# A graph-network kernel on one Trainium2 core: the first mixer's key sums taken apart from its queries

## The chip, the cores and the metric

The kernel runs on one core of one Trainium2 chip. The metric is device microseconds from launch to the end, lower is better. The program is one launch: five engines (TensorE, VectorE, ScalarE, GpSimd, SyncE; in the profile PE, DVE, ACT, POOL, SP) each work through their own instruction list in order and wait for each other by semaphores.

## The reference, cut to what matters

The network has two layers over 3125 nodes of 256 features (25 tiles of 128 nodes, the last one partly filled) and 53125 edges. Only the first layer's first step is touched by the change:

```python
xn = layernorm(x)
x = x + gnn(xn, src, dst, edge_weight) + mixer(xn)       # first layer, first step
x = x + experts(layernorm(x))                            # first layer, 32 experts, one chosen per node
# second layer: relational attention over the edges, a second mixer, a routed network
```

The graph part sums, for each node, `xn[src] * edge_weight` over its edges and multiplies by a weight. The mixer makes `q, k, v` from `xn`, norms q and k over the features and squares them, norms again (the keys' second norm is over the nodes, so it is known only when all nodes are summed), and needs `k.T @ v` over all nodes before any node's result is known:

```python
q2, k2 = square(norm(q)), square(norm(k))     # norm over a node's features
out = (q2 / |q2| per node) @ (k2.T @ v / |k2| per feature) @ W_out
```

The sum over nodes does not depend on the order of the nodes.

## The kernel before

**The head (`prepare`).** The nodes are read in node order (`xs`, 25 tiles). The head finds each node's first edge and its number of edges and sorts the nodes by it: the rank is called the node's *place*. The search runs in five rounds: VectorE makes row numbers (L969 to L973), GpSimd issues five indirect DMAs for them (L976), VectorE counts in what they brought (L980). Then comes one chain of VectorE and TensorE steps (L991 to L1039). Beside all this, the layernorm of each tile `xn` is made (L115 to L119) and written to a table `xtab` in HBM (L1045). The head ends with a flag that all engines load, and a branch: an engine enters the next stage only when its part of the head is done.

**The front (`front`).** After the branch, tile t holds the nodes of places 128t to 128t+127. GpSimd first gathers two edge windows (L1273) and the node rows by place (`xs`, L1570). Weights are loaded through ScalarE's DMA queue: 4 MB for the experts, then those of the mixer, its biases `b_qkv` last. Three streams are then woven together in the order of the program; ScalarE, VectorE and TensorE keep exactly this order (`manual_schedule`), while GpSimd's is set by the scheduler:

- `first_mixer`, a pipeline over 25 tiles. Per tile: layernorm (`norm1`, `norm2`), the transpose of `xn` (`turn`), three products (`products`: queries 256 wide, keys and values 512 wide, a direct part 256 wide), the norms and squares (`squares1`, `squares2`), and `sums`: the transpose of `q2` into `q2T`, `kvT += v.T @ k2` and `sqs += k2*k2`. It yields twice per tile. After the last tile come the scale `cn` and the matrix `kvo` (L1531 to L1547).
- `summing` (called `slots`): the graph part. A tile has as many *slots* as its node with the most edges, `SLOTS = [38, 25, 23, 22, 21, 20, 20, 19, 19, 18, 18, 17, ...]`, 444 in all. One step takes four slots: four indirect DMAs on GpSimd (L1384, tile `g`, four buffers of four slots) and four multiply-adds on VectorE (L1389, L1391). Two more steps per tile transpose the sum and multiply it by the weight (L1399 to L1403).
- `sources` (called `counts`): lists for the last network of the second layer, 32 blocks of 6 steps, mainly VectorE (L1151 to L1194).

The weaving in the mixer is this:

```python
while step is not None:
    at += 1
    if at > 6:
        slots()
        counts(step)      # the mixer yields 0, 1, 0, 1, ...: every second time
    step = next(mixer, None)
```

Then the experts run over 7 groups of four tiles (`chosen`, `experts`, `projections`). A group has 32 half steps. Each calls `more`, which makes one step of `slots` (at most up to the end of the group after next), issues one indirect scatter of the finished lists on GpSimd (L1240, two once all slots are done) and makes one step of `counts`. Before a group's experts start, `slots(NT * 99, ...)` finishes all slots of that group and of the next: the first group needs tiles 0 to 7. Lists can be scattered only when 8 blocks of `counts` are complete.

**The second layer** follows the front: gathers of `kvtab` (L1929), attention, and the routed network.

Of the kernel before, what the change touches and what calls it, by code (L numbers as in the profile page):

```python
# [12 lines left out]
F32 = mybir.dt.float32  # L13
BF16 = mybir.dt.bfloat16
I32 = mybir.dt.int32
AF = mybir.ActivationFunctionType
OP = mybir.AluOpType
# [4 lines left out]
P = 128  # L22
N = 3125
D = 256
KB = D // P
NT = 25
NP = NT * P
# [4 lines left out]
E2 = 32768  # L32
C2 = E2 // P
NTAB = 2
TR = NP + P
# [12 lines left out]
GS = 40  # L48
# [3 lines left out]
def rows(t):  # L52
    return P if t < NT - 1 else LAST
# [843 lines left out]
class Fast(Net):  # L897
# [32 lines left out]
    def prepare(self, ctx):  # L930
        tc, nc, a = self.tc, self.nc, self.a
        keep = ctx.enter_context(tc.tile_pool(name="pr_keep", bufs=1, reuse_waits="tile"))
# [8 lines left out]
        self.place = keep.tile([P, 2, NT], F32, name="place_of")  # L941
        flag = keep.tile([1, 1], I32, name="flag")
        self.ones3 = keep.tile([3, P], BF16, name="ones3")
        nc.vector.memset(self.ones3, 1.0)
        self.later = keep.tile([3, 2], F32, name="later")
        for k in range(2):
            nc.vector.tensor_scalar(self.later[:, k:k + 1], self.iotap[:3], float(k), -1.0, op0=OP.is_gt,
                                    op1=OP.mult)
        with ExitStack() as ctx:
# [7 lines left out]
                           allow_small_or_imprecise_dtypes=True)  # L957
# [82 lines left out]


            for t in range(NT):
                xn = work.tile([P, D], F32, name="xn")
                self.layernorm(work, self.xs[:, t, :], xn)
                nc.sync.dma_start(self.xtab[t * P:(t + 1) * P, :], xn)  # L1045
        return nc.values_load(flag, min_val=0, max_val=2 * P)

# [62 lines left out]
    def sources(self, ctx):  # L1110

        tc, nc, a = self.tc, self.nc, self.a
        B = 8
# [11 lines left out]
        slot = one.tile([P, C2], F32, name="slot2")  # L1125
        over = one.tile([P, C2], F32, name="over2")
        other = one.tile([P, C2], F32, name="other2")
        nc.gpsimd.iota(other, pattern=[[P, C2]], base=NP * GS, channel_multiplier=1,
                       allow_small_or_imprecise_dtypes=True)
        self.placed_chunks = 0  # L1130
# [15 lines left out]
        for b in range(C2 // B):  # L1146
# [48 lines left out]
            if b % 8 == 7:  # L1195

                cs = slice((b - 7) * B, (b + 1) * B)
                nc.vector.tensor_scalar(over[:, cs], slot[:, cs], float(GS), None, op0=OP.is_ge)
                nc.vector.scalar_tensor_tensor(slot[:, cs], dst[:, cs], float(GS), slot[:, cs],
                                               op0=OP.mult, op1=OP.add)  # L1200
                nc.vector.tensor_sub(other[:, cs], other[:, cs], slot[:, cs])
                nc.vector.tensor_mul(other[:, cs], other[:, cs], over[:, cs])
                nc.vector.tensor_add(self.sidx2[:, cs], slot[:, cs], other[:, cs])
                self.placed_chunks = (b + 1) * B
# [26 lines left out]
    def source_lists(self, n, to=None):  # L1231
# [7 lines left out]
        for c in range(len(done), min(len(done) + n, self.placed_chunks)):  # L1239
# [11 lines left out]
            done.append(ins)  # L1251
        self.last_scatters = done[-NCH:]

    def neighbours(self):
# [150 lines left out]

    def first_mixer(self, ctx, q2T, nq, kvo):

# [29 lines left out]
        kvT = ps.tile([P, KB, D], F32, name="kvT")  # L1437
        sqs = big.tile([P, D], F32, name="sqs")
        nc.vector.memset(sqs, 0.0)
        sd = {}  # L1440
        made = {}
        squared = {}
        xns = {}
        xTs = {}

        def norm1(t):
# [17 lines left out]
        def products(t):  # L1464
            xT = xTs.pop(t)
            pqv = ps.tile([P, 2, D], F32, name="pqv", bufs=2)
            pkv = ps.tile([P, 2 * D], F32, name="pkv", bufs=2)
            self.mm_rows(pqv[:, 0], xT, w_q, b_qkv[:, 0:D])
            self.mm_rows(pkv, xT, w_kv, b_qkv[:, D:])
            self.mm_rows(pqv[:, 1], xT, w_vo, b_vo)  # L1470
            made[t] = pqv, pkv

        def squares1(t):

            pqv, pkv = made[t]
            st = work.tile([P, 2, 6], F32, name="mx_st")
            mv = work.tile([P, 2, 2], F32, name="mx_mv")
            r = work.tile([P, 3, 2], F32, name="mx_sd")
            nc.vector.bn_stats(st[:, 0, :], pqv[:, 0])
            nc.vector.bn_stats(st[:, 1, :], pkv[:, 0:D])  # L1480
            for k in range(2):
                nc.vector.bn_aggr(mv[:, k, :], st[:, k, :])
            nc.scalar.activation(r[:, 0, :], mv[:, :, 1], AF.Sqrt, bias=self.eps[:, 1:2],
                                 scale=float(D))
            made[t] = pqv, pkv, mv, r

        def squares2(t):
            pqv, pkv, mv, r = made.pop(t)
            nc.vector.reciprocal(r[:, 1, :], r[:, 0, :])
            nc.vector.scalar_tensor_tensor(r[:, 2, :], mv[:, :, 0], -1.0, r[:, 1, :],  # L1490
                                           op0=OP.mult, op1=OP.mult)
            q2 = work.tile([P, D], F32, name="q2")
            k2 = work.tile([P, D], F32, name="k2")
            v = work.tile([P, D], F32, name="v")
            sq = work.tile([P, 2, D], F32, name="sq", bufs=2)
            nc.scalar.activation(q2, pqv[:, 0], AF.Square, bias=r[:, 2, 0:1], scale=r[:, 1, 0:1])
            nc.scalar.activation(k2, pkv[:, 0:D], AF.Square, bias=r[:, 2, 1:2],
                                 scale=r[:, 1, 1:2])
            nc.scalar.copy(v, pkv[:, D:])
            nc.vector.tensor_add(self.xs[:, t, :], self.xs[:, t, :], pqv[:, 1])  # L1500
            nc.scalar.activation(sq[:, 0, :], q2, AF.Square, accum_out=nq[:, t:t + 1])
            nc.scalar.activation(sq[:, 1, :], k2, AF.Square)
            squared[t] = q2, k2, v, sq

        def sums(t):
            q2, k2, v, sq = squared.pop(t)
            r = rows(t)
            self.transpose_to(ps, q2, q2T[:, :, t * P:(t + 1) * P])
            for k in range(KB):
                nc.tensor.matmul(kvT[:, k, :], v[:r, k * P:(k + 1) * P], k2[:r, :],  # L1510
                                 start=(t == 0 and k == 0), stop=(t == NT - 1 and k == KB - 1))
            nc.vector.tensor_add(sqs[:r], sqs[:r], sq[:r, 1, :])

        def there(f, t):
            if 0 <= t < NT:
                f(t)

        for t in range(-2, NT + 2):
            there(turn, t + 1)
            there(sums, t - 2)  # L1520
            there(products, t)
            there(norm1, t + 2)
            there(squares1, t - 1)
            yield 0
            there(norm2, t + 2)
            there(squares2, t - 1)
            yield 1

        kv = big.tile([P, KB, D], F32, name="kv")
        for k in range(KB):  # L1530
            nc.vector.tensor_copy(kv[:, k, :], kvT[:, k, :])  # L1531
        cn = work.tile([1, D], F32, name="cn")
        csum = ps.tile([1, D], F32, name="pqv", bufs=2)
        nc.tensor.matmul(csum, self.ones[:, 0:1], sqs, start=True, stop=True)
        nc.scalar.activation(cn, csum, AF.Sqrt)
        nc.vector.tensor_scalar_max(cn, cn, 1e-12)
        nc.vector.reciprocal(cn, cn)
        pc = ps.tile([P, KB], F32, name="pqv", bufs=2)
        for k in range(KB):
            nc.tensor.matmul(pc[:, k:k + 1], cn[:, k * P:(k + 1) * P], self.ones[0:1, 0:1],  # L1540
                             start=True, stop=True)
        rc = work.tile([P, KB], F32, name="rc")
        nc.vector.tensor_copy(rc, pc)
        for c in range(KB):
            pw = ps.tile([P, D], F32, name="pqv", bufs=2)
            self.mm_rows(pw, kv[:, :, c * P:(c + 1) * P], w_o)
            nc.vector.tensor_scalar(kvo[:, c, :], pw, rc[:, c:c + 1], None, op0=OP.mult)  # L1547
        nc.scalar.activation(nq, nq, AF.Sqrt)
# [4 lines left out]
    def front(self, q2T, qT, kvtab, own):  # L1553
# [5 lines left out]
        with ExitStack() as ctx:  # L1559
# [3 lines left out]
            nq = big.tile([P, NT], F32, name="nq")  # L1563
            kvo = big.tile([P, KB, D], F32, name="kvo")
            w_y = self.load_kb(big, "w_y", a["gcn_wT"])
# [29 lines left out]
            def counts(n=1):  # L1595
                for _ in range(n):
                    next(counted, None)

            self.edges_of(0)
            with ExitStack() as mctx:  # L1600
                mixer = self.first_mixer(mctx, q2T, nq, kvo)
                step = next(mixer)
                mctx.enter_context(tc.manual_schedule(
                    engines={mybir.EngineType.Activation, mybir.EngineType.DVE, mybir.EngineType.PE}))
                at = 0
                while step is not None:
                    at += 1
                    if at > 6:
                        slots()
                        counts(step)  # L1610
                    step = next(mixer, None)
# [821 lines left out]
```

## Time and profile before

| what | value |
|---|---|
| median of 17 runs | 2488.05 us (2483.55 to 2495.62) |
| the profiled execution | 2488.35 us, its span 2486.6 us |
| head, up to the flag (L1039) | 0 to 98.8 us |
| first norm of a query tile (L1479) | 149.55 us |
| last slots step before the experts (L1403, tile 7) | 453.46 us |
| first activation of the experts (L1709) | 456.14 us |
| first gather of the second layer (L1929) | 1258 us |

A line of the profile names the source line, the engine, what is written from what, and the shapes; `x444` is a count. "Busy" is the time that an engine executes; the idle time before an instruction is put down to what released it. PEclk is the granted clock of TensorE. In the timetables of stretches, the columns are the length and then, for each engine, busy time and number of instructions.

### The profile page before, as it was taken

How to read it: one execution, taken by the hardware profiler on the slowest of the kernel's cores; microseconds unless marked ns; L12 is line 12 of the kernel's file. 1: busy time of each engine (PE TensorE's matmuls, PEld its weight loads, DVE VectorE, ACT ScalarE, POOL GpSimd, SP SyncE). 2: the span in 40 equal slices, each digit the busy share in tenths (PEclk: the TensorE clock that was granted, in tenths of full speed). 3: DMA queues.
4: the chain of work that ended last, by engine and by line, in shares of the span. 5: the costliest groups of instructions: out<-in, count | busy, mean ns of one | idle time of the engine just before them, and what ended most of it. 6: DMA issues, size and time to landing. Idle time of an engine off the chain costs nothing.

```text
span 2486.6 us, 25047 instructions
## 1 busy us (share of the span) xinstructions
PE 1786.7 (72%) x7318; PEld 1113.9 (45%) x7318; DVE 1480.9 (60%) x4053; ACT 783.2 (31%) x2273; POOL 1588.5 (64%) x1675
## 2 busy tenths in 40 slices
PE   0177785677887889999837565756575658888898
PEld 0034443444444545555525343534354425555556
DVE  6566768866666565531468687978677823122227
ACT  1023331111121212222306443535454423332342
POOL 3376556777777776467357777767654037777764
PEclk9998886888899899999968776778767669999999
DMA  4443223432333332101167576756655031111101
GB/s 148 130 136 113 83 80 113 120 88 86 104 97 100 94 98 78 43 18 35 38 176 208 152 215 201 215 175 202 191 143 164 12 98 17 17 17 9 17 10 53
DMA packets 121375, 254.50 MB, mean 102 GB/s; under 512 B 36594, under 2 KB 61926, under 8 KB 120972
## 3 DMA queue, kind: packets, MB, share of 16 engines
q0 software_dynamic: 82656, 196.67, 28.5%
q1 hardware_dynamic: 31688, 49.09, 5.9%
q10 hardware_dynamic: 6884, 7.04, 1.0%
q8 instruction: 60, 0.98, 0.2%
q14 instruction: 87, 0.71, 0.1%
HBM read 228.93 MB, written 23.76 MB: 102 GB/s over the span
## 4 chain that ended last, share of the span: by engine, by line
POOL 13%; DVE 10%; PE 10%; issue 8%; DMA 5%; ACT 4%; DVEq 0%; POOLq 0%; ACTq 0%
POOL ed L2140 7%; DMA kv<-kvtab,src 4%; POOL kv L1929 3%; ACT kv L1966 3%; DVE kv L1937 2%; DVE kv L1935 2%; PE po L2279 2%; PE pu L1968 2%; PE ph L2267 2%; DVE sc L1938 2%; PE pz L926 1%; DMA ed<-htab,nb 1%; POOL hx L2107 1%; PE pr L1368 1%; PE pT L126 1%
## 5 line engine op out<-in xcount | busy, mean ns | idle before, releaser
L1384 POOL DMA_INDIRECT g<-xtab,src x444 | 445.1, 1002 | 188.0 <-issue 108.8
L1929 POOL DMA_INDIRECT kv<-kvtab,src x444 | 431.0, 971 | 183.0 <-issue 99.9
L2140 POOL DMA_INDIRECT ed<-htab,nb x279 | 265.0, 950 | 85.0 <-issue 81.0
L1240 POOL DMA_INDIRECT gl<-gsrc,sidx x256 | 255.8, 999 | 79.1 <-issue 76.8
L1966 ACT ACTIVATE kv<-kv,sc 128x64 f32<-128x64 f32 x1196 | 288.2, 334 | 21.5 <-DVE sc L1950 21.4
L1968 PE MATMUL pu<-kv,ident 128*128 128x256 f32 x888 | 259.1, 434 | 11.8 <-ACT kv L1966 9.9
L1391 DVE SCALAR_TENSOR_TENSOR acc<-g,wt,acc 128x256 f32<-128x256 f32 x419 | 202.8, 484 | 61.6 <-DMA g<-xtab,src 51.0
L2267 PE MATMUL ph<-xT,w 128*128 128x512 f32 (+1 forms) x448 | 191.1, 581 | 35.9 <-ACT h L2269 26.5
L1706 PE MATMUL ph<-xT,w 128*128 128x512 f32 (+1 forms) x448 | 214.8, 605 | 0.0
L1723 PE MATMUL po<-w,h 128*128 128x256 f32 x800 | 204.6, 397 | 0.0
L1968 PEld LDWEIGHTS pu<-kv,ident 128*128 128x128 f32 x888 | 175.6, 214 | 59.6 <-ACT kv L1966 37.2
L2279 PE MATMUL po<-w,h 128*128 128x256 f32 x800 | 187.0, 386 | 0.0
L2279 PEld LDWEIGHTS po<-w,h 128*128 128x128 f32 x800 | 148.9, 191 | 33.4 <-issue 15.4
L1723 PEld LDWEIGHTS po<-w,h 128*128 128x128 f32 x800 | 148.4, 196 | 34.2 <-issue 17.6
L1935 DVE TENSOR_TENSOR kv<-kv,pr 128x1024 f32<-128x1024 f32 (+3 forms) x121 | 133.2, 1123 | 46.6 <-DMA kv<-kvtab,src 32.0
L1709 ACT ACTIVATE h<-ph,b 128x512 f32<-128x512 f32 (+1 forms) x112 | 71.7, 640 | 265.0 <-PE ph L1707 265.0
L2267 PEld LDWEIGHTS ph<-xT,w 128*128 128x128 f32 x448 | 84.1, 201 | 124.6 <-issue 94.6
L1354 PE MATMUL pT<-typT,sel 18*128 18x128 bf16 (+9 forms) x229 | 32.1, 270 | 149.0 <-DVE typT L1345 146.9
L1937 DVE TENSOR_TENSOR kv<-kv,q 128x1024 f32<-128x1024 f32 (+3 forms) x121 | 132.3, 1122 | 0.0
L1938 DVE TENSOR_REDUCE sc<-kv 128x16 f32<-128x1024 f32 (+3 forms) x121 | 132.1, 1119 | 0.0
L1368 PE MATMUL pr<-self.relb,ohT 128*128 128x128 bf16 x687 | 79.2, 268 | 46.2 <-DVE ohT L1357 37.6
L1706 PEld LDWEIGHTS ph<-xT,w 128*128 128x128 f32 x448 | 82.2, 206 | 55.4 <-issue 53.9
(443 smaller groups left out, 2947.7 us busy)
## 6 DMA issues: line engine op xcount, KB each, us to landing
dr<-in_gat_dst_row SPq DMA_DIRECT2D x32, 512.0 KB, 3.9
g<-xtab,src POOLq DMA_INDIRECT x444, 2.8
kv<-kvtab,src POOLq DMA_INDIRECT x444, 3.7
own<-xq SPq DMA_DIRECT2D x25, 256.0 KB, 2.0
xq<-own SPq DMA_DIRECT2D x25, 256.0 KB, 3.2
ed<-htab,nb POOLq DMA_INDIRECT x279, 2.4
w<-in_ex_w ACTq DMA_DIRECT2D x2, 2048.0 KB
gl<-gsrc,sidx POOLq DMA_INDIRECT x256, 2.1
```

The lines of the kernel that those rows point to most:

```text
L1240: ins = nc.gpsimd.indirect_dma_start(out=self.gl[:, :], out_offset=bass.IndirectOffsetOnAxis(ap=self.sidx2[:, c:c + 1], axis=0), in_=self. ...
L1384: self.moved = nc.gpsimd.indirect_dma_start(out=g[:, s % 4, :], out_offset=None, in_=self.xtab[:, :], in_offset=bass.IndirectOffsetOnAxis( ...
L1391: nc.vector.scalar_tensor_tensor(acc, g[:, s % 4, :], self.wts[t][:, s:s + 1], acc, op0=OP.mult, op1=OP.add)
L1706: nc.tensor.matmul(ph[:, :n], w1[:, k, mc], xT[:, k, :n], start=(k == 0), stop=False)
L1723: nc.tensor.matmul(pos[j // 2][:, j % 2], this[:, j * P:(j + 1) * P], w2[:, m, :], start=False, stop=(m == M - 1 and (j % 2 == 1 or j == w ...
L1929: nc.gpsimd.indirect_dma_start(out=kv[:, j, :], out_offset=None, in_=kvtab[:, :], in_offset=bass.IndirectOffsetOnAxis(ap=self.srcs[t][:, g ...
L1935: nc.vector.tensor_tensor(k4, k4, rr[:, r0:r0 + n].unsqueeze(2).to_broadcast([P, n, 4, HD]), op=OP.add)
L1966: nc.scalar.activation(v[:, h * HD:(h + 1) * HD], v[:, h * HD:(h + 1) * HD], AF.Copy, scale=sc[:, s, h:h + 1])
L1968: nc.tensor.matmul(pu, self.ident, v, start=(s == 0), stop=(s == SLOTS[t] - 1))
L2140: nc.gpsimd.indirect_dma_start(out=ed[:, s, :], out_offset=None, in_=self.htab[:, :], in_offset=bass.IndirectOffsetOnAxis(ap=self.nbrs[t][ ...
L2267: nc.tensor.matmul(ph[:, :w], w1[:, e, k, m * P:(m + 1) * P], xT[:, :len(ts), k, :], start=(k == 0), stop=(k == KB - 1))
L2279: nc.tensor.matmul(po[:, i], hs[i][:, m, j * P:(j + 1) * P], w2[:, e0 + i, m, :], start=False, stop=(i == 1 and m == M - 1))
```

## The change

The mixer's keys no longer go with its queries. Since the sum over the nodes takes them in any order, the keys and values of the first 12 tiles in node order are made and summed in the head, next to the layernorm that makes `xn` there; the sums are kept in `kvs` and `cs`. After the branch the mixer first reads back `xtab` for node tiles 12 to 24, makes their keys and adds their sums. Only then do the queries run, by places, over all 25 tiles. The columns' squares are now summed by a matmul (`csum`) and no longer by VectorE (`sqs`). The scale and `kvo` (now in `kvs`) are made in four steps during the queries. The weaving changes: the mixer yields 0 twice per key tile, then 1 and 2 per query tile; every yield makes a step of `counts`, and only a 2 makes a step of `slots`.

The weights `w_kv` and the key biases are loaded once more for the head. Of the buffers of `sources`, two small ones are made anew every 8 blocks.

```diff
+NHEAD = 12
 # prepare
+            w_kv = self.load_kb(one, "w_kv", a["mix0_wkv"])
+            b_kv = self.load_terms(one, one, "b_kv", a["mix0_b"][D:])
+            def keys(t, xn):
+                xT = work.tile([P, KB, P], F32, name="xT", bufs=2)
+                self.transpose_to(ps, xn, xT)
+                pkv = ps.tile([P, 2 * D], F32, name="pkv", bufs=2)
+                self.mm_rows(pkv, xT, w_kv, b_kv)
...
+                r = self.key_norm(work, pkv)
+                self.key_squares(pkv, r, k2, v, sq)
+                return k2, v, sq
             for t in range(NT):
-                xn = work.tile([P, D], F32, name="xn")
+                xn = work.tile([P, D], F32, name="xn", bufs=8)
                 self.layernorm(work, self.xs[:, t, :], xn)
                 nc.sync.dma_start(self.xtab[t * P:(t + 1) * P, :], xn)
+                if t < NHEAD:
+                    now = t, *keys(t, xn)
+                if last:
+                    self.key_sums(kvT, csum, *last, 0, NHEAD - 1)
+            nc.scalar.copy(self.kvs, kvT)
+            nc.scalar.copy(self.cs, csum)
 # new helpers
+    def key_norm(self, work, pkv):
+        nc.vector.bn_stats(st, pkv[:, 0:D])
+        nc.vector.bn_aggr(mv, st)
+        nc.scalar.activation(r[:, 0:1], mv[:, 1:2], AF.Sqrt, bias=self.eps[:, 1:2], scale=float(D))
+        nc.vector.tensor_copy(r[:, 3:4], mv[:, 0:1])
+    def key_squares(self, pkv, r, k2, v, sq):
+        nc.vector.reciprocal(r[:, 1:2], r[:, 0:1])
+        nc.vector.scalar_tensor_tensor(r[:, 2:3], r[:, 3:4], -1.0, r[:, 1:2], op0=OP.mult, op1=OP.mult)
+        nc.scalar.activation(k2, pkv[:, 0:D], AF.Square, bias=r[:, 2:3], scale=r[:, 1:2])
+        nc.scalar.copy(v, pkv[:, D:])
+        nc.scalar.activation(sq, k2, AF.Square)
+    def key_sums(self, kvT, csum, t, k2, v, sq, first, last):
+        for k in range(KB):
+            nc.tensor.matmul(kvT[:, k, :], v[:r, k * P:(k + 1) * P], k2[:r, :],
+                             start=(t == first and k == 0), stop=(t == last and k == KB - 1))
+        nc.tensor.matmul(csum, self.ones[:r, 0:1], sq[:r, :], start=(t == first), stop=(t == last))
 # first_mixer
-        for t in range(-2, NT + 2):
-            there(turn, t + 1)
-            there(sums, t - 2)
+        for t in range(NHEAD - 1, NT + 2):
+            those(fetch, t + 2 if t + 2 > NHEAD + 1 else -1)
+            those(turn, t + 1)
+            those(sums, t - 2)
+            those(keys, t)
+            those(squares_k1, t - 1)
+            there(norm1, t + 1 - NT)
+            yield 0
+            those(squares_k2, t - 1)
+            there(norm2, t + 1 - NT)
+            yield 0
...
+        for t in range(0, NT + 2):
+            there(turn, t + 1 if t else -1)
...
+            there(turned, t - 2)
             there(products, t)
-            there(norm1, t + 2)
+            there(norm1, t + 2 if t else -1)
             there(squares1, t - 1)
-            yield 0
-            there(norm2, t + 2)
+            yield 1
+            there(norm2, t + 2 if t else -1)
             there(squares2, t - 1)
-            yield 1
+            scale(t - 4)
+            yield 2
 # front
                 while step is not None:
-                    at += 1
-                    if at > 6:
+                    if step == 2:
                         slots()
-                        counts(step)
+                    counts()
                     step = next(mixer, None)
```

`fetch` reads one tile of `xtab` back through SyncE; `keys`, `squares_k1`, `squares_k2` and `sums` do for a key tile what the helpers say; `those` runs them for tiles 12 to 24 alone; `turned` transposes `q2`; `scale` makes the scale and `kvo`, one part per tile from tile 4 on. `products`, `squares1` and `squares2` keep their query parts.

## The prediction

> **What bounds the kernel now.** I read the page's slices first, then a timetable of the front by its own stages, then what GpSimd and VectorE wait for in it. From the page, where each digit is the busy share of 62 us:
>
> ```profile
> PE   0177785677887889999837565756575658888898
> DVE  6566768866666565531468687978677823122227
> POOL 3376556777777776467357777767654037777764
> PEclk9998886888899899999968776778767669999999
> ```
>
> Slices 2 to 20 are the front, 99 to 1258 us; the change touches nothing behind. GpSimd shows a 7 through most of it and never more. The timetable says what a 7 is. Its stages are the mixer (137 to 401 us), the step between (401 to 453), and expert groups 0 to 4 and the rest:
>
> ```profile
> 137.00:401.00 264.00, 206.30 (x743) 116.72 (x742) 186.20 (x634) 87.67 (x269) 170.52 (x172) 0.86 0.33 96
> 401.00:453.00 52.00, 21.01 (x104) 14.95 (x105) 43.98 (x146) 6.81 (x16) 35.59 (x36) 0.55 0.39 114
> 453.00:580.00 127.00, 96.44 (x439) 57.37 (x438) 95.04 (x327) 20.89 (x40) 96.53 (x95) 0.87 0.33 97
> 580.00:725.00 145.00, 117.05 (x480) 68.20 (x478) 88.87 (x316) 29.11 (x61) 111.48 (x111) 0.89 0.34 104
> 725.00:864.00 139.00, 113.28 (x488) 65.99 (x487) 84.30 (x303) 30.84 (x63) 106.84 (x106) 0.90 0.30 92
> 864.00:994.00 130.00, 111.86 (x487) 65.49 (x487) 84.00 (x312) 30.46 (x63) 90.32 (x90) 0.96 0.29 88
> 994.00:1101.00 107.00, 100.50 (x434) 58.59 (x432) 49.25 (x194) 27.77 (x57) 55.30 (x57) 1.00 0.11 35
> ```
>
> From 500 to 700 us, GpSimd issues 39 indirect DMAs in nearly every 50 us, 1.28 us each, and waits for almost nothing. What it waits for from 453 to 990 us (columns: total us, times, longest):
>
> ```profile
> POOL g L1384 <- issue: 60.9, 200, 0.3
> POOL gl L1240 <- issue: 38.1, 125, 0.3
> POOL g L1384 <- DVE src L1295: 6.2, 3, 4.3
> POOL kvtab L1756 <- DVE scr L1176: 5.1, 4, 4.2
> ```
>
> The 0.3 us "issue" after each DMA is part of its price: about 1.0 us busy and 0.3 us behind it. So groups 0 to 3 are GpSimd's: 95, 111, 106 and 90 DMAs at 1.28 us are 122, 142, 136 and 115 us of 127, 145, 139 and 130. From group 4 on TensorE is the bound (100.5 of 107 us). In the mixer GpSimd has time to spare: 172 DMAs are 220 of 264 us. It waits there for VectorE, which must consume a slot before its buffer is free. VectorE's own waits in the mixer:
>
> ```profile
> DVE xs L1403 <- PE sums L133: 22.2, 5, 7.3
> DVE xs L1500 <- ACT q L1496: 21.0, 25, 5.8
> DVE xs L1403 <- PE g L1168: 7.9, 1, 7.9
> ```
>
> One reading governs the sum: through group 3 the time is that of GpSimd's DMAs, and a stage that makes too few slots leaves it idle for good.
>
> **The head.** Per key tile VectorE gets a norm (0.41 and 0.17 us, L1480 and L1482), a 1-column copy (0.15, L1078), a reciprocal and a product (0.16 each, L1489 and L1490): 1.05 us, or 0.95 net of a tenth that successive instructions overlap (from 150 to 385 us the groups' sums exceed the 169.9 busy by about that). Twelve tiles are 11.4 us, and the bias split (L912 to L914, for 768 columns 0.75 + 1.0 + 0.5 + 1.0 + 0.5) about 2.5 at 512. VectorE has 99 - 69.4 = 30 us idle in the head: 8 before the first x lands, 15.9 in front of the counting steps L980, 5 in the last chain, which runs from 70 to 99 us and is otherwise dense. In the changed program's order five key tiles (4.8 us) and about 34 layernorm instructions (some 8 us), which before stood in the gaps ahead of 63 us, stand in that chain. Of these 13 us about 4 find its gaps: +9. TensorE's key work is 4.5 us a tile by the mixer's rows net of overlap (two transposes 0.4, four halves of the 512-wide product 2.0, bias 0.3, kvT 1.2, and csum, not in the trace, 0.2 by a bias matmul or 0.6 by half a kvT, taken as 0.6). That is 54 us beside the 75 between about 22, when x and `w_kv` can be in, and 97; but it stands in the queue ahead of the chain's g2a matmuls: +3. ScalarE's 2.0 us a tile (copy 0.37, root 0.29, squares 0.56 and 0.42, copy 0.37) are 24 us where it was busy for 8: hidden. Sum +12. Ends: +4 if the gaps take all but the dense part, +25 if TensorE is late.
>
> The lateness has a row: in the head a 400-column bf16 matmul (L1075) took 499 ns, in the mixer a 512-column one (L927) 384, though the granted clock of the head reads 9 tenths and more in the page. By that ratio, 1.25 to 0.75 ns a column, the 54 us become up to 90, more than the 75 there are; I take the middle, 72, since a loaded TensorE need not stay so slow.
>
> The Trainium skill, "TensorE: Matmul & The Clock Gate", Part 1, speaks against this part: TensorE idles at half clock and gets the full one only after some 3.4 us of sustained work. By it, scattered key matmuls would all run at half rate, 108 us as an estimate, and the head would end some 30 us late instead of 12. The row agrees with the rule and not with the clock shown.
>
> **From the flag to the first norm.** Before, 98.8 to 149.55 us: VectorE waits 20.4 us for `b_qkv`, last in the queue of loads. Nothing of it is removed: keys of tile 12 need the same `w_kv` and `b_qkv`. Reading `xtab` adds 128 KB per tile to SyncE, two tiles of it in this time, beside 236 GB/s: 1 us, hidden. First key norm at 149.6 + 12 = 162.
>
> **The 13 key tiles.** TensorE per tile: 4.5 us and two counts steps at 0.2 each, 4.9. VectorE: 0.95 and two counts steps. From 453 to 990 us 22 blocks cost 158 us in the groups L1151 to L1194, 6.5 net a block, 1.08 a step: 3.1 in all. So TensorE sets 5.0 us a tile (4.3 with its clock at 1.00 instead of 0.88): 12 periods are 60 us, and the last two sums, `kvs` and the first query products 10 more. First query norm at 232. No slots are made here. GpSimd fills its 16 buffered slots and stops.
>
> **The 25 query tiles.** VectorE per tile: two norms (0.42 + 0.18 + 0.40 + 0.17), two reciprocals, one product, `xn` 0.42, the add into xs 0.42, less overlap 2.2; one slots step, 86 slots in 27 steps at 0.48 = 1.5, and `edges_of` and the tile sums 0.3; two counts steps 2.15. Sum 6.2. The wait for ScalarE in front of L1500 stays (21.0 over 25 tiles: 0.8). Period 7.0; ends 6.2 (no wait) and 8.8 (the mixer's present ratio, 264 to 186). TensorE needs 4.6 and GpSimd 3.2 x 1.28 = 4.1, both less. 24 periods are 168 us, first norm to last, and two closing steps 10: the mixer ends at 410. Before, it ended at 401 after `kvo`, whose serial 390 to 399 us are spared here: they lie inside the 168.
>
> **What is owed.** Before, 58 yields less 6 made 52 steps: tiles 0 to 5 were done, 390.24 us. Now 27 steps: tiles 0 to 2 (38 + 25 + 23 = 86 slots). Tiles 3 to 7 hold 102, of which 16 sit in buffers. GpSimd must issue 86 and 5 windows, 91 x 1.28 = 117 us, and the last one's landing, sum and product take about 7. The step between (52 us of `chosen`) fits beside. Group 0 starts at 410 + 124 = 534 instead of 453.5: **+81**. These lines are the two ends of that stage before:
>
> ```profile
> 390.24 0.42 DVE L1403 TENSOR_TENSOR xs<-xs,sums 128x256 f32<-128x256 f32 x1 [0.53 <-PE sums L133]
> 453.46 0.42 DVE L1403 TENSOR_TENSOR xs<-xs,sums 128x256 f32<-128x256 f32 x1 [0.69 <-PE g L1173]
> ```
>
> **Later.** The counts are 61 steps further on (87 in the mixer instead of 26). Lists are ready when group 0 starts, so it issues 32 scatters instead of 23: 9 x 1.28 = 12 us of GpSimd's time, of which the group's own slack (127 - 122) takes 5: +7. In return no counts are left in group 4, the first that TensorE bounds: 24 steps at 0.2 = -5. In group 3 the relief lies beside GpSimd and is worth nothing. The iota of 256 columns becomes four of 64 in GpSimd's queue; each waits for counts that stand well ahead of the slots queued behind it: 0. Total 81 + 7 - 5 = **+83**. The profiled execution took 2488.35 us, 1.75 more than its span and 0.3 above the median; the forecast is 2571.
>
> **The rivals.** *TensorE is the bound, and the gathers follow.* Then the change gains: 12 x 3.5 = 42 us of products and sums leave the front, and the `kvo` block's 9; 13 extra transposes and csums (0.4 + 0.6) cost 13, the head 12. 2488 - 26 = 2462. For it speaks that TensorE is busy 206 of 264 us in the mixer and 22 us of VectorE's waits there are for it; against, that groups 0 to 3 have GpSimd at its pace. It decides if group 0 starts before 451 us, so if the mixer ends by 327: queries at 3.5 us a tile, little over half of VectorE's work. Chance 0.05, and 0.02 for a draw.
> *The slots are nearly caught up.* With VectorE never waiting (-19), a key tile at 4.3 us (-8) and the head at +4 (-8) the time is 2536, still inside the forecast's range. To come below 2525 and stay above 2493 the 117 us owed would have to shrink too, by GpSimd issuing faster than the 1.28 us of every row. Chance 0.08.
> *The queries go at the old ratio.* 8.8 us a tile (+43) and the head at +25 (+13): 2627. Above 2615: 0.07.
>
> **The numbers.** The forecast, 2525 to 2615, keeps 0.78; this is also the range. A measurement can tell about 0.2% (5 us) from no change. Faster 0.05, same 0.02, slower 0.78 + 0.08 + 0.07 = 0.93.
>
> **What would show it.** The flag near 111 us; GpSimd nearly silent between about 165 and 230; L1403's third entry, not its sixth, near the mixer's end at about 410; a solid row of gathers to about 530, TensorE idle and its clock near 0.5; groups 0 to 3 about as long as before, group 0 by some 10 us longer; L1929 first near 1340. Wrong would be: first experts before 480 us, query tiles under 6 us, or group times that shrink.

## The result and the profile after

The changed kernel takes 2557.9 us (median of 8 runs, 2555.6 to 2562.2); the kernel before took 2489.2 us beside it. The ratio is 1.0277, with a 95% interval of 1.0263 to 1.029: 69 us slower. The forecast was 2571 us in a range of 2525 to 2615. The profiled execution took 2563.45 us, its span is 2561.6. The last four of the twelve experiments were measured on another chip (chip 0; the first eight on chip 4), where the kernel before took 3229 us instead of 2490, so their times are compared with its time there alone.

In the changed file the lines are shifted: the gathers L1384 are L1441, their multiply-adds L1391 are L1448, the last slots step L1403 is L1460, the lists' scatters L1240 are L1269, the first activation of the experts L1709 is L1792, and the wait L1500 is L1565.

The page's slices of after, 64 us a digit:

```profile
PE   5468774256777889999973755766676648997898
DVE  6748787755665755312238867978867742122127
POOL 3242347777777777757517777776746117777763
PEclk9777675577889999999985877777867668998999
```

TensorE now works in the head (slices 1 and 2). GpSimd shows 2 to 4 in slices 4 to 6, where it had 5 and 6, and then goes at 7 as before; TensorE falls to 4 and 2 in slices 7 and 8, where it had 5 and 6. The timetable of after, by its own stages (key phase, queries, what is owed, then groups 0 to 3; columns are length, then PE, PEld, DVE, ACT and POOL busy with counts, granted clock, DMA share, GB/s):

```profile
159.00:230.00 71.00, 63.10 (x298) 30.42 (x297) 51.24 (x235) 28.39 (x79) 10.38 (x12) 0.93 0.22 70
230.00:413.00 183.00, 132.95 (x563) 80.82 (x562) 150.22 (x557) 65.85 (x193) 86.49 (x84) 0.66 0.29 88
413.00:540.00 127.00, 34.52 (x139) 23.63 (x140) 84.02 (x260) 7.33 (x18) 96.99 (x101) 0.50 0.39 113
540.00:686.00 146.00, 102.50 (x422) 63.27 (x421) 88.59 (x299) 20.96 (x39) 112.49 (x111) 0.81 0.30 86
686.00:830.00 144.00, 116.83 (x484) 69.56 (x483) 89.44 (x312) 29.88 (x61) 111.23 (x110) 0.91 0.35 104
830.00:964.00 134.00, 110.23 (x473) 66.31 (x471) 83.92 (x299) 30.14 (x61) 102.80 (x103) 0.92 0.31 93
964.00:1075.00 111.00, 103.59 (x360) 59.83 (x359) 49.45 (x149) 25.01 (x52) 84.60 (x87) 0.95 0.26 75
```

In the key phase GpSimd issues 12 DMAs in 71 us, in the queries 84 in 183. The third row is the debt: 101 DMAs in 127 us, TensorE busy 34 of it. The two ends of that stretch, the third and the eighth of the last slots steps:

```profile
415.21 0.42 DVE L1460 TENSOR_TENSOR xs<-xs,sums 128x256 f32<-128x256 f32 x1 [1.72 <-PE sums L134]
539.89 0.42 DVE L1460 TENSOR_TENSOR xs<-xs,sums 128x256 f32<-128x256 f32 x1 [3.51 <-PE sums L134]
```

Tile 2 is summed when the mixer ends and tile 7 at 540 us, where the kernel before had tile 5 and 453. What GpSimd waits for from 540 to 1075 us (total us, times, longest):

```profile
POOL g L1441 <- issue: 64.6, 212, 0.3
POOL gl L1269 <- issue: 39.3, 129, 0.3
...
POOL g L1441 <- DVE acc L1448: 2.4, 8, 0.3
```

Only the 0.3 us behind each DMA is left; the 11.3 us that GpSimd waited for VectorE before, in the third and fourth lines of the prediction's list, are gone. And in the mixer's queries VectorE waits for ScalarE as it did:

```profile
DVE xs L1565 <- ACT q L1564: 19.1, 25, 3.3
```

The first activations of the seven groups, from the trace:

| | group 0 | 1 | 2 | 3 | 4 | 5 | 6 |
|---|---|---|---|---|---|---|---|
| before, us | 456.1 | 579.7 | 725.3 | 864.5 | 993.8 | 1101.3 | 1189.8 |
| after, us | 543.5 | 688.8 | 832.6 | 966.5 | 1077.3 | 1175.6 | 1264.1 |
| length before | 123.6 | 145.6 | 139.2 | 129.2 | 107.5 | 88.5 | |
| length after | 145.3 | 143.8 | 133.9 | 110.9 | 98.2 | 88.5 | |

Group 0 starts 87 us later, its own length grows by 22, groups 1 to 4 shrink by 2, 5, 18 and 9. What remains at group 6 is +74, and the profiled executions differ by 75.

### The profile page after: what moved, and what is told of

It reads as the page before. It is cut to its first block, busy times and chain, and to the rows that moved or that the text cites. A ratio compares the mean times of both kernels' runs of the same rounds, so it can differ in the third digit from the quotient of the medians.

```text
span 2561.6 us, 25422 instructions
## 1 busy us (share of the span) xinstructions
PE 1854.9 (72%) x7416; PEld 1147.4 (45%) x7416; DVE 1486.5 (58%) x4107; ACT 804.8 (31%) x2326; POOL 1589.6 (62%) x1678
## 5 line engine op out<-in xcount | busy, mean ns | idle before, releaser
L1441 POOL DMA_INDIRECT g<-xtab,src x444 | 447.3, 1008 | 264.2 <-issue 111.5
L2012 POOL DMA_INDIRECT kv<-kvtab,src x444 | 431.5, 972 | 183.0 <-issue 101.7
L1269 POOL DMA_INDIRECT gl<-gsrc,sidx x256 | 253.4, 990 | 78.0 <-issue 77.7
L1448 DVE SCALAR_TENSOR_TENSOR acc<-g,wt,acc 128x256 f32<-128x256 f32 x419 | 203.0, 484 | 110.8 <-DMA g<-xtab,src 101.8
L1806 PE MATMUL po<-w,h 128*128 128x256 f32 x800 | 220.8, 421 | 0.0
L2350 PE MATMUL ph<-xT,w 128*128 128x512 f32 (+1 forms) x448 | 190.7, 580 | 36.6 <-ACT h L2352 26.5
L1789 PE MATMUL ph<-xT,w 128*128 128x512 f32 (+1 forms) x448 | 201.6, 574 | 0.0
L2362 PE MATMUL po<-w,h 128*128 128x256 f32 x800 | 186.9, 386 | 0.0
L1806 PEld LDWEIGHTS po<-w,h 128*128 128x128 f32 x800 | 158.4, 209 | 33.3 <-issue 13.3
L2362 PEld LDWEIGHTS po<-w,h 128*128 128x128 f32 x800 | 148.9, 191 | 33.4 <-issue 15.5
L2018 DVE TENSOR_TENSOR kv<-kv,pr 128x1024 f32<-128x1024 f32 (+3 forms) x121 | 133.1, 1122 | 43.9 <-DMA kv<-kvtab,src 29.4
L1792 ACT ACTIVATE h<-ph,b 128x512 f32<-128x512 f32 (+1 forms) x112 | 71.6, 640 | 225.3 <-PE ph L1790 225.3
L1425 PE MATMUL pr<-self.relb,ohT 128*128 128x128 bf16 x687 | 79.4, 268 | 43.1 <-DVE ohT L1414 34.4
```

The lines of the kernel that those rows point to most:

```text
L1269: ins = nc.gpsimd.indirect_dma_start(out=self.gl[:, :], out_offset=bass.IndirectOffsetOnAxis(ap=self.sidx2[:, c:c + 1], axis=0), in_=self. ...
L1441: self.moved = nc.gpsimd.indirect_dma_start(out=g[:, s % 4, :], out_offset=None, in_=self.xtab[:, :], in_offset=bass.IndirectOffsetOnAxis( ...
L1448: nc.vector.scalar_tensor_tensor(acc, g[:, s % 4, :], self.wts[t][:, s:s + 1], acc, op0=OP.mult, op1=OP.add)
L1789: nc.tensor.matmul(ph[:, :n], w1[:, k, mc], xT[:, k, :n], start=(k == 0), stop=False)
L1806: nc.tensor.matmul(pos[j // 2][:, j % 2], this[:, j * P:(j + 1) * P], w2[:, m, :], start=False, stop=(m == M - 1 and (j % 2 == 1 or j == w ...
L2012: nc.gpsimd.indirect_dma_start(out=kv[:, j, :], out_offset=None, in_=kvtab[:, :], in_offset=bass.IndirectOffsetOnAxis(ap=self.srcs[t][:, g ...
```

## The experiments

The theory: GpSimd's DMAs set the front's time, and the change keeps slots from GpSimd in the mixer; they are owed behind it. The rival: the chain itself (a head with keys, a key phase, then the queries) has become longer, and slots fit in anywhere. The change also makes 87 counts steps in the mixer instead of 26, a third suspect. "Tile" below is the period of a query tile (first to last norm, by 24), T0 the first activation of group 0.

**Half the slots in the kernel before.**

```diff
 # before: 26 slots steps in the mixer instead of 52
-                        slots()
+                        slots(step)
```

> The kernel before, with slots made at every second yield of the mixer only (26 steps instead of 52); nothing else is changed. Theory 'withheld slots': the front's time is that of GpSimd's DMAs, and steps withheld in the mixer are owed behind it. VectorE saves 26 steps of about 1.5 us, so the mixer ends near 361 us instead of 400; tiles 0 and 1 and most of tile 2 are done; some 95 DMAs are owed, 95 x 1.28 = 122 us and 7 for the last sum. Group 0 starts near 490 instead of 456, and the time is near 2526 us (2510 to 2545). Rival 'order and head': the loss of the change comes from its longer chain (a head with keys, a key phase of its own, then the queries), and slots fit in anywhere. Then this kernel is no slower than before: 2450 to 2490.

Measured: 2512.9 us, ratio 1.0072 [1.0048, 1.0095]; the tile 7.08 us instead of 9.61, T0 473.5 instead of 456.1. Slower although every tile of the mixer became 2.5 us shorter: slots that are withheld cost time with no other part of the change. But the price is 18 us and not 37, because a slots step was worth 2.5 us of a tile and not 1.5. GpSimd's longest waits in this mixer make the cause visible:

```profile
POOL g L1384 <- DVE ed L1287: 36.1, 2, 18.2
```

L1287 begins the next tile's edge lists, and VectorE does it right behind the multiply-adds of a tile's first slots step: in one case three L1391 ran from 237.90 us for 1.52 us, the first L1287 ended at 239.64 and the gather followed at 239.69. So GpSimd goes on when VectorE takes up a new tile's first step; whether the buffers or the edge lists release it comes to the same step. The two closing steps of a tile take no slots, and GpSimd stands still through them: 18 us at one step per tile of the mixer, at most 9.6 at two steps (before).

**The changed kernel with other weavings.** Three edits of the same four lines:

```diff
 # slots_both
-                    if step == 2:
+                    if step:
                         slots()
 # counts_few
-                    counts()
+                    if step == 2:
+                        counts()
 # split_only: both of these
```

> The changed kernel, with a slots step at both yields of a query tile (54 steps, about the 52 of before). Withheld slots: a query tile takes 7.2 + 1.5 = 8.7 us, the mixer ends near 450 instead of 413, but then only some 14 DMAs are owed instead of 91, group 0 starts near 478 instead of 543, and the time falls by about 60 to 2496 us (2480 to 2525). Order and head: the chain is as long as it was, so the time stays within 20 us of the changed kernel, 2540 or more.

> The changed kernel, with counts only at a query tile's second yield (27 steps in the mixer instead of 87, about the 26 of before). Withheld slots: the queries' VectorE time falls by 1.1 us a tile and the key phase stays TensorE's, so group 0 starts some 30 us earlier; lists come later, so group 0 has fewer scatters and is 10 to 20 us shorter; but the counts return to groups 3 and 4, which lose their gain of 19 and 9 us. About 2535 us (2515 to 2560). If the counts lie in gaps anyway, nothing moves: 2558. If group 3's gain of 19 us does not come from the counts, groups 3 and 4 keep 111 and 98 us.

> The changed kernel, woven as before: a slots step at both yields of a query tile (54, before 52) and a counts step at every second one (27, before 26). It differs from the kernel before in the split of the keys alone. Theory 'the split has a price of its own': keys beside queries cost VectorE's tile little (7.08 us a tile with keys against 6.32 without, both with one slots and one counts step), but the key phase costs 44 us and the head 9. Then a query tile takes 9.4 - 1.1 = 8.3 us, the mixer ends near 420 instead of 400, group 0 starts near 478 instead of 456, and the time is 2512 us (2500 to 2525). Rival 'only what is withheld counts': as slots and counts are those of before, the time is that of before plus the head's 9 us at most: 2485 to 2500.

| kernel | slots steps | counts steps | tile, us | T0, us | ratio to before |
|---|---|---|---|---|---|
| before | 52 | 26 | 9.61 | 456.1 | 1 |
| split_only | 54 | 27 | 8.41 | 475.4 | 1.0044 [1.0029, 1.0059] |
| slots_both | 54 | 87 | 9.40 | 517.8 | 1.0126 [1.0100, 1.0152] |
| counts_few | 27 | 27 | 6.33 | 503.3 | 1.0176 [1.0149, 1.0202] |
| after | 27 | 87 | 7.22 | 543.5 | 1.0277 [1.0263, 1.0290] |

Read from split_only to counts_few to after, the 69 us come apart: the split alone 0.44% (11 us), half of the slots 1.3% (33), the 60 thicker counts 1.0% (25). On the other way through slots_both the counts are 0.8% and the slots 1.5%. Neither theory is the whole. The slots are the largest part; the rival's price is there, but small; the counts, which I had put inside the lengths of the phases, are a part of the loss as large as a third.

At T0 the three parts are 19, 28 and 40 us, 87 in all. The counts lose 40 there; group 0 lasts 12 us longer with them, and groups 3 and 4 give 25 back (131.4 and 102.8 us with 27 counts, 110.9 and 98.2 with 87). Group 3, in TensorE's waits and the timetable, first before and then after:

```profile
PE g L1168 <- DVE lo L1157: 9.5, 4, 3.8
PE g L1189 <- DVE sums L1183: 2.1, 4, 1.2
...
864.52:993.77 129.25, 111.11 (x485) 65.10 (x486) 83.28 (x307) 30.23 (x63) 89.93 (x90) 0.96 0.29 89
```

```profile
PE sums L1456 <- DVE acc L1448: 4.5, 2, 3.2
...
966.47:1077.34 110.87, 103.46 (x357) 59.70 (x358) 49.45 (x150) 25.01 (x52) 84.41 (x87) 0.95 0.26 75
```

Counts feed TensorE products (L1168, L1189) that stand in its ordered queue ahead of the experts: it waits 11.6 us for VectorE's part of them and is busy 7.7 us longer; 111.1 us busy and 18.1 of waits in all fill the 129.2. GpSimd waits for VectorE too, 10.7 us in this group, nearly all of the 11.3 named above. With the counts made earlier group 3 takes 110.9 us, which is 87 DMAs at 1.28 us (111): only now it is GpSimd's. counts_few has the same wait back (12.6 us for L1182).

The split's own price: the first query norm comes at 213.4 us, 64 later than the first norm of before, and a query tile without keys is only 1.2 us shorter (29 us over 24 tiles). Alone the keys take 3.84 us a tile in split_only, and TensorE is busy in all of these 46.1 us; with the two counts steps of the changed kernel it is 4.64. Beside queries most of that time did not show.

**Slots from the key phase on.**

```diff
-                    if step == 2:
+                    at += 1
+                    if at > 17:          # the last 16 yields of the key phase too
                         slots()
```

> The changed kernel, with a slots step at each of the last 16 yields of the key phase and at both yields of a query tile (70 steps). Withheld slots: VectorE has some 20 us idle in the key phase, so that becomes at most 15 us longer; the queries go at 8.7 us a tile; the mixer ends near 465 with tiles 0 to 7 done, group 0 starts near 485, and GpSimd is 5 steps (26 us) further than before was at that point. With the gain in groups 3 and 4 kept, about 2472 us (2450 to 2500), at or below the kernel before. Order and head: 2540 or more.

Measured: 2517.2 us, 1.0097 [1.0071, 1.0123]: 41 us better than the change, 45 worse than I expected. Tile 7 is summed at 471.0 us, as planned, but T0 is 526.3. Now the mixer ends last (last query norm 472.5), and group 0's own start behind it, a serial chain of products, norms and routing (`chosen`), takes the 54 us. The lead of slots shortens group 0 to 115.9 us, but not the groups behind (141.4, 134.7, 111.1): a group makes slots only up to the end of the group after next, so each of these still issues a whole group's DMAs (106, 102 and 87).

**No counts in the mixer of the kernel before.**

```diff
                         slots()
-                        counts(step)
```

> The kernel before without counts in the mixer (26 steps less); they are made in the groups. From the two kernels with 87 and 27 counts in the mixer: 60 steps moved group 0's start by 40 us and the sum of the groups by 13 the other way. For 26: group 0 starts 17 us earlier, the groups grow by 6, and lists that are late leave some scatters to the end of the front. 2480 us (2470 to 2492). If GpSimd sets the mixer's pace in this kernel, nothing moves there and the time is 2489 or more.

Measured: 2458.2 us, 0.9864 [0.9846, 0.9881]: faster than both kernels, by 32 and 100 us, and faster than I expected. The tile is 8.62 us, T0 431.5 (25 earlier for 26 steps), groups 0 and 1 are 6 and 12 shorter, groups 4 and 5 8 and 9 longer. GpSimd's waits at L1287 are half of before's 31.7 us:

```profile
POOL g L1384 <- DVE ed L1287: 15.2, 4, 4.6
```

The change went the other way with the counts.

**More keys in the head.**

```diff
-NHEAD = 12
+NHEAD = 20
```

> The changed kernel with 20 key tiles in the head instead of 12, and 5 instead of 13 in the key phase. Measured for 12: the flag 9.3 us later, 0.78 us a tile; the key phase 4.64 us a tile. If the head goes on at 0.78, the flag comes 6 us later and the key phase is 37 shorter: 2527 us. TensorE was busy 66 of the changed head's 108 us, some 59 of them with keys, 4.9 us a tile; 8 more are 39, so the head becomes TensorE's and the flag comes 10 to 20 us later: 2541 us, which is my figure (2525 to 2557). No gain at all (2558 or more) would say that a key tile costs the head as much as the key phase.

Measured: 2545.6 us, 1.0223 [1.0204, 1.0241]. The time is near my figure, and so is the reason, but not at the flag. The flag stands at 107.6 us, where it stood with 12 tiles (106.9 to 108.1 in these kernels), since the last key tiles queue behind the chain that makes it. An engine passes the branch only when its own part of the head is done, though: with 12 tiles all five did at 108.3 us, here GpSimd and SyncE do at 107.8, VectorE at 129.9, TensorE at 131.3 and ScalarE at 133.1. VectorE waits 15.4 us for key products in the head, and then for the mixer's biases, which ScalarE's queue loads behind the branch; its last key norm in the head and the end of that wait are

```profile
128.67 0.43 DVE L1289 BATCH_NORM_STATS2 mk_st<-pkv 128x6 f32<-128x256 f32 x1 [4.18 <-PE pkv L928]
...
172.41 0.55 DVE L913 CAST b_qkv<-b_qkv_f 3x768 bf16<-3x768 f32 x1 [21.86 <-DMA b_qkv_f<-in_mix_b]
```

With 12 tiles the biases came at 149.1 us. So the key phase starts 23 us later (first norm at 181.9 instead of 158.9) and is 36.6 us shorter, as forecast (19.1 us from its first to its last norm instead of 55.7). The difference is what the first query norm gains: 216.5 instead of 229.8 us. A key tile beyond the twelfth costs the head 23 / 8 = 2.9 us, since the head is then TensorE's (busy 20.1 of the 23.3 us from 108 to 131.3).

**The wait for the biases.**

```diff
 # before: experts' and router's loads issued behind next(mixer)
-            w_r = self.load_kb(fe, "w_r", a["route_wT"])
...
                 step = next(mixer)
+                w_r = self.load_kb(fe, "w_r", a["route_wT"])
...
```

> The kernel before, with the loads of the router's and experts' weights (4 MB) issued behind the mixer's instead of ahead of them. VectorE waited 20.4 us for the mixer's biases, last in that queue. If the wait is those 4 MB, the first norm comes 15 to 20 us earlier, at about 132, all that follows is earlier by as much, and the time is 2472 us (2465 to 2482). If something else is late as well (the node rows by place, the other weights), the gain is under 8 us.

Measured: 2489.7 us, 0.999 [0.9979, 1.0002]: nothing. The wait did fall from 20.4 to 7.8 us and the first norm came 10 us earlier, at 139.4:

```profile
DVE b_qkv L912 <- DMA b_qkv_f<-in_mix_b: 7.8, 1, 7.8
...
DVE acc L1391 <- DMA g<-xtab,src: 10.8, 15, 1.2
```

The second line is from the stretch behind it (139 to 205 us): VectorE now waits 10.8 us for gathers, 2.7 before. GpSimd issues the 25 gathers of node rows ahead of the first slots, 1.25 us each from 102.6 to 134.5 us, and the first `g` leaves at 136.3 us, 0.8 earlier than before. The wait moved to GpSimd, where the front's time is.

**Four that tell little.** These are the four measured on chip 0. The edits: the changed kernel with slots at both yields and no counts (12, then 20 key tiles in the head), the change with `NHEAD = 4`, and the kernel before with `counts(1 + step)` at every yield.

> The changed kernel with a slots step at both yields of a query tile and no counts in the mixer; counts go to the groups. It stands to the kernel before without counts (2458 us) as split_only stands to the kernel before. Theory 'each part has its own price': the split costs 11 us as it did there, so about 2470 us (2460 to 2482). Rival 'the split and the counts hurt each other, both through VectorE': without counts the split is free or gains, 2458 or less.

> The same with 20 key tiles in the head instead of 12. With the changed weaving 8 more key tiles in the head were worth 12 us: the flag did not move, and TensorE finished the head's keys behind the branch, until 132 us, while VectorE waited for the mixer's biases. The same gain makes about 2459 us (2450 to 2472), the best that the split can give here. If the front is by now GpSimd's from its first gather on, the earlier queries wait for gathers and the gain is under 5 us: 2465 or more.

> The changed kernel with 4 key tiles in the head instead of 12. 8 tiles more in the key phase are 8 x 4.64 = 37 us; if the head's 9 us are made of key tiles' VectorE steps, it gets back 5 of them: 2590 us (2578 to 2602). If keys in the head cost as much as in the key phase: 2565 or less. If the flag stays near 108, the head's 9 us do not come from the key tiles but from layernorms that were moved into its last chain.

> The kernel before with 87 counts steps in the mixer instead of 26 (one at each first yield, two at each second), as many as the changed kernel has; keys and slots as before. Leaving 26 out moved group 0's start by 24.6 us, 0.95 a step. If that price holds, 61 more are 58 us; groups 3 and 4 give back about 28 as in the changed kernel: 2520 us (2505 to 2545). If counts are dear only where VectorE has no keys and queries to wait for, the time is below 2500; if they make VectorE the pace of the whole mixer and give nothing back, 2550.

Measured, against 3228.8 us: 1.0012 [0.9977, 1.0047], 1.0016 [0.9991, 1.0041], 1.0113 [1.0080, 1.0147] and 1.0105 [1.0043, 1.0168]. In counts_before GpSimd and VectorE are busy as long as in the kernel before on chip 4 (1576 and 1486 us against 1588 and 1481), TensorE 133 us longer (1920 against 1787), but behind the branch engines stand for some 10 us at a time, and the profile names nothing that ends the wait (`remote`); two of ScalarE's lines (100 to 1300 us):

```profile
ACT xT L127 <- remote: 119.3, 9, 19.2
...
ACT h L1709 <- remote: 114.8, 12, 24.9
```

A change of 30 us does not stand out from 740 us more, and the cause of the stalls stays open: nothing here tells the chip from anything else that was different there. So it is open whether the split is free once the counts are gone. The second expectation takes TensorE to have carried keys across the branch in nhead20, which the loads of the flag above rule out. Only the flag can be read, since in counts_before (99.0 us) it is that of before: with 4, 12 and 20 key tiles the flag stood at 102.1, 103.6 and 108.0 us there, and with 20 VectorE passed the branch only at 154.9.

## Why the prediction was right, and where it was not

The sign, the place and the size held: +83 forecast, +69 measured in medians and +75 in the profiled executions.

- *Flag +12:* +9.3, mostly for the reason given, VectorE. From the last counting step to the flag it took 29.6 us before and 38.0 after; VectorE was busy 23.5 us of it before and 31.3 after, its waits for TensorE were 5.1 and 6.6, and key norms stand in the chain:

```profile
80.48 0.99 DVE L1106 TENSOR_TENSOR_SCAN place<-g2a,nothing 128x400 f32<-128x400 f32 x1 [2.17 <-PE g2a L1104]
81.39 0.41 DVE L1289 BATCH_NORM_STATS2 mk_st<-pkv 128x6 f32<-128x256 f32 x1
```

  The end of +25, a late TensorE, did not come with 12 tiles, where TensorE passed the branch at 108.3 us with the others. With 20 tiles it did: 131.3 us, though the flag had not moved.
- *TensorE in the head, 54 to 90 us, taken as 72:* the key work's groups sum to 65 us there. The first four `kvT` products took 2.08 us, the next four at 36.76 us 1.13, and the 400-column matmul 333 ns, where before it took 499.

```profile
31.70 2.08 PE L1307 MATMUL kvT<-k,v 128*128 128x256 f32 x4
...
36.76 1.13 PE L1307 MATMUL kvT<-k,v 128*128 128x256 f32 x4
```

  The Trainium skill's "TensorE: Matmul & The Clock Gate", Part 1, has the rule that a cold TensorE runs at half rate; these two rows agree with it, and the granted clock beside them does too, 0.50 from 30.95 to 34.3 us and 1.00 from 34.4 to 47.9. The prediction set the clock of before's head against the rule, but the trace of before holds no record of the clock ahead of 140.2 us, and the profile's page counts such a stretch as full speed. My estimate from the rule, 108 us with every key cold, did not come: busy for 30 of the 40 us from 20 to 60 at a granted clock of 0.87, TensorE made its 512-wide key products in 695 ns there and in 617 in the key phase.
- *First norms:* keys 162, queries 232 forecast; 159 and 230 measured. The key period was 4.64 us, inside 4.3 to 5.0.
- *Query period 7.0, mixer's end 410:* 7.22 and 413. A term in it was mis-sized: a slots step is worth 2.1 to 2.5 us of a tile (three pairs of kernels) and not 1.5. A counts step is worth 0.9 to 1.0 (two pairs) and not 1.08, which takes back some of it.
- *Group 0 at 534, +81:* its first activation came at 543.5, +87. The debt is there as told, 101 DMAs in 127 us where I had 91 in 117.
- *Group 0 +7:* +22; this step failed. The scatters came as told (32 for 24). But there are also 9 more gathers: before, 14 slots of tile 8 lay in the buffers when the group began, after only 6, since a GpSimd that is late finds its buffers empty. 18 DMAs more, 23 us. I had counted 16 buffered slots as paid at the debt's start and not that they are owed again at its end.
- *Group 3, 0:* -18; this step failed. I gave groups 0 to 3 to GpSimd on sums of 122, 142, 136 and 115 us beside 127, 145, 139 and 130, and passed over the last pair's 15 us. They were TensorE's waits for counts, 11.6 us, and GpSimd's waits for VectorE, 10.7 us, which stood in my own list of waits as the lines that I called almost nothing. *Group 4, -5:* -9, for the same reason.
- The rivals: *TensorE is the bound* is out; relieving TensorE of keys per tile bought 1.2 us of each. *The old ratio* of 8.8 us a tile did not come: VectorE's wait for ScalarE stayed at 0.8 us a tile.

The misses, +6 at T0, +15 in group 0 and -30 in groups 1 to 4, leave -9: they met by luck, and the good figure owes something to that. And the text named one cause, withheld slots, where the runs show three: they are half of it, the counts a third.

## What to carry to other kernels

When one engine's DMAs set the time of a long stage, price an edit by how long it leaves that engine idle ahead of the stage, whichever engine causes it: here the split, the missing slots and the thicker counts all did, and an earlier start that did not reach GpSimd was worth nothing. Before giving a stage to an engine, compare the sum with its length; here a gap of a tenth was a wait for another engine, and side work that feeds an ordered queue was behind it. Splitting a pipeline into two phases with different bounds gives up the overlap between them: keys cost 1.2 us a tile beside queries and 3.8 alone. And a flag tells when it was made, not when the engines reach the branch behind it: look at each engine's own load of it.

## What the runs showed that I had not expected

- Leaving 26 counts steps out of the mixer of the kernel before gains 32 us, more than the 28 us of VectorE's time that I had given them, with nothing else removed: they are only made later, in groups that have room.
- The flag is not the end of the head: with 20 key tiles it stood where it did with 12, and yet VectorE, TensorE and ScalarE passed the branch 22 to 25 us later, while GpSimd went ahead.
- The profile prints a granted clock of 1.00 for 140 us of the kernel before in which the trace holds no record of it; the durations (499 ns for a 400-column matmul, 333 in the changed head) are what shows the slow head.
